# A graph attention layer and its neighbours: the counting of adj spread over 91 steps, the order of chunks in the first and last half head changed, and layer 3's dense stage reordered

## The chip, the cores and the metric

One NeuronCore of one Trainium2 chip. The metric is the device time of one execution in microseconds, as the median of several runs. Engines are named as in the profile: PE (matrix engine; PEld is its weight load), DVE (vector), ACT (scalar, activation functions), POOL (GpSimd), SP (the queue that issues most DMAs).

## The reference

Four graph layers on the same graph, each `x = x + layer(relu(layernorm(x)), adj)`. `x` is 2708 x 512 in float32, `adj` 2708 x 2708 in int32 with zeros and ones, symmetric, with ones on the diagonal. The change concerns layer 2 and the start of layer 3:

```python
def layer2(x, adj, W, a1, a2):           # 8 heads of 64
    Wh = einsum('nd,hdo->hno', x, W)
    f1, f2 = einsum('hno,ho->hn', Wh, a1), einsum('hno,ho->hn', Wh, a2)
    e = leaky_relu(f1[:, :, None] + f2[:, None, :], 0.2)
    att = softmax(where(adj > 0, e, -9e15), axis=-1)
    return elu(einsum('hnm,hmo->hno', att, Wh))   # heads side by side: n x 512

def layer3(x, adj, W_self, b_self, W_nb, b_nb, W_comb, b_comb):
    agg = mask @ x / max(deg, 1)
    both = concatenate([x @ W_self + b_self, agg @ W_nb + b_nb], -1)
    return relu(both @ W_comb + b_comb)
```

Layer 0 is relu of a degree-normalized `adj.T @ X @ W`; layer 1 averages each node's first 64 neighbours and adds a dense part.

## The kernel before, in words

The 2708 nodes are cut into 22 chunks of up to 126 rows (`NC` = 22, `R` = 126; the last one has 62). Layer 0 leaves the transposed adjacency on the chip as int8, six tiles `vT`. Each layer has a dense stage, chunk by chunk (load, normalize, transpose, multiply), and an aggregation over pairs of chunks. All matrix products are in float32 or its one-pass form except where bf16 is named.

**Layer 2, dense** (L655 to L735). `dense` gives load, normalize, transpose, multiply with lags 0 to 3; `product2` multiplies by the weights of all heads, stores the result `wh` to DRAM as `whd`, and multiplies it by the rows `a1` on DVE and `a2` on POOL (L666, L672); `sums2` reduces them to f1 and f2; `rows2` transposes f1 to a row that goes to DRAM (`rT`). `exps2` (L701) takes exp of f2 in two forms on ACT (`ef`, `ec`), and on POOL makes `eb` and splits `ef` and `ef*ec` into three bf16 parts each (`parts`, `parts2`): 13 small operations, once for the first 11 chunks (`EARLY`) during the dense stage and once for the rest in attention.

**Layer 2, attention** (L803 to L1019). The eight heads are ten units: the first and last head are cut in two halves of the target nodes (1384 and 1324 columns), the others have all 2708. Each unit has 22 steps, one per source chunk m: 220 steps. The softmax's weights are factored, so that a step is

- `make` (L858, DVE): `t2 = max(rb, ec) * vT`, one instruction over all columns, into one of four tiles; up to three steps ahead;
- `scale` (L831, L833, ACT): the step's 64 columns of Wh times `ef`, as `whs`; for the chunks not in `BY_SIDE` also a column for the sum of weights;
- `compare` (L843, ACT), only for the 13 chunks in `BY_SIDE` (m % 5 in 1, 3, 4): from `t2` a 0/1 pattern `b` in bf16 by a steep sigmoid;
- `multiply` and `multiply_sides` (L882, PE): `av += whs.T @ t2` in 4 column groups of 32; the sums of weights from `t2` in float32 (chunks not in `BY_SIDE`), or from `b` with `parts` in bf16 (the others), the latter one step later.

`load_wh` fetches three chunks' slices of `whd` at a time, six steps ahead. Work beside the steps is put behind step numbers in `plan`: loads and exp of the next head's row `rb` (L642, L649), `evict` of a unit's results to DRAM (`avT`, `sumT`) at its end, and `count_neighbors` (L932) behind steps 66 to 78, one chunk of `BY_SIDE` each: four ACT conversions of a quarter of the chunk's int8 adjacency to bf16 (L941), into tiles of the x ring (six), and eight matmuls (L946) with `parts2`. The last steps get layer 3's first loads and turns.

**Layer 3, dense** (L747 to L801, L1022 to L1061). For chunk c: `load3` (aT, sT and x from DRAM), `turn3` (sums_ps L766 and av_ps L770 on PE; then rs and y on DVE, L772 to L777), `elu3` (z on POOL L784; th and z with tanh and exp on ACT L787, L788; L785, L789, L790 on DVE), `save3` (x to DRAM from ACT's queue), `normalize3` (statistics L187, L189, square root on ACT L191, L192 and hn L201 on DVE), `transpose3` (hT_ps L210 on PE, hT L212 on ACT), `product3` (nb_ps and self_ps, L182 on PE; halves L249, L251; y L1045, stored from ACT's queue). `staged` runs them in one program order with lags 0, 1, 2, 3, 4, 4, 5 for load, turn, elu, normalize, save, transpose, multiply.

The order of instructions on each engine is fixed when the program is built: a list scheduler starts from the program order above and from its own costs, and semaphores are added where engines meet. Within an engine the instructions run in that order, a waiting one holds up what stands behind it.

Of the kernel before, what the change touches and what calls it, by code (L numbers as in the profile page):

```python
# [44 lines left out]
def fast_layers(  # L45
# [59 lines left out]
    KMAX = max(sizes)  # L105
    EARLY = NC // 2
# [152 lines left out]
    def load_x(src, c, name="x", pool=None, bufs=6, twice=False):  # L259
        n = rows(c)  # L260
        t = (pool or common).tile([P, D], F32, name=name, bufs=bufs)
        if twice and c == NC - 1:
            nc.gpsimd.memset(t[:R], 0.0)
            move(nc.sync, t[TAIL : TAIL + n, :], src[c * R : c * R + n, :])
        move(nc.sync, t[:n], src[c * R : c * R + n, :])
        return t
# [383 lines left out]

    l2p = ctx.enter_context(ExitStack())
# [49 lines left out]
    def exps2(cs):  # L701
        nc.scalar.activation(ef[:, cs], f12[:R, cs, H:], AF.Exp)
        nc.scalar.activation(ec[:, cs], f12[:R, cs, H:], AF.Exp, scale=SLOPE2 - 1.0)
        nc.gpsimd.tensor_scalar(eb[:, cs], ec[:, cs], -STEEP * ABOVE, None, op0=ALU.mult)
        size = cs.stop - cs.start
        rest = cp.tile([R, EARLY, H], F32, name="rest")[:, :size]
        for i, e in enumerate((ef, ec)):
            if i:
                nc.gpsimd.tensor_tensor(rest, ec[:, cs], ef[:, cs], ALU.mult)
                e = rest  # L710
            else:
                e = ef[:, cs]
            for k in range(3):
                part = parts_of[:, cs, :, 3 * i + k]
                nc.gpsimd.tensor_copy(part, e)
                if k < 2:
                    nc.gpsimd.tensor_tensor(rest, e, part, ALU.subtract)
                    e = rest
        nc.gpsimd.tensor_copy(
# [6 lines left out]
    def rows2(c):  # L726
# [4 lines left out]
        if c == NC - 4:  # L731
            exps2(slice(0, EARLY))
            exp_row(*units[0])

    staged(NC, *dense(x2, product2, False, [(4, sums2), (5, rows2)], scalar=True))  # L735

    ws = load_weight(weights, fused[0], "wfs", tag="w")
    wn = load_weight(weights, fused[1], "wfn", tag="w")
# [5 lines left out]
    kept3 = {}  # L744

# [57 lines left out]
    with ExitStack() as stack:  # L803
        at = stack.enter_context(tc.tile_pool(name="att", bufs=1, reuse_waits="tile"))
        weight, wh, whs, acc, sides = {}, {}, {}, {}, {}
        steps = [(u, m) for u in range(len(units)) for m in range(NC)]


        GROUP = 3

        def load_wh(s):
            u, m = steps[s]
            h = units[u][0]
            t = at.tile([R, GROUP, O], F32, name="wh", bufs=3)
            k = min(GROUP, NC - 1 - m)
            if k > 0:
                src = whd[m * R : (m + k) * R, h * O : (h + 1) * O]
                nc.sync.dma_start(t[:, :k], src.rearrange("(k p) o -> p k o", p=R))
            if k < GROUP and m + k == NC - 1:
                src = whd[(NC - 1) * R :, h * O : (h + 1) * O]  # L820
                nc.sync.dma_start(t[:last_rows, k], src)
            for j in range(GROUP):
                wh[u, m + j] = t[:, j]

        def scale(s):

            u, m = steps[s]
            h, q = units[u][0], rows(m)
            t = at.tile([R, O + S], F32, name="whs", bufs=4)
            by = ef[:q, m, h : h + 1]  # L830
            nc.scalar.activation(t[:q, :O], wh.pop((u, m))[:q], AF.Copy, scale=by)  # L831
            if m not in BY_SIDE:
                nc.scalar.activation(t[:q, O:], one6[:q], AF.Copy, scale=by)  # L833
            whs[s] = t
# [43 lines left out]
        def four(out, size, operands, m):  # L878

            for p, (a, b) in zip(out, pieces(size)):  # L880
                for j, (lhsT, rhs, part) in enumerate(operands):
# [4 lines left out]
                        start=(m == 0),  # L886
                        stop=(m == NC - 1),
                    )

        def multiply(s):  # L890
# [3 lines left out]
            if m == 0:  # L894
# [6 lines left out]
            four(acc[u][0], half, [(cols[j % 2], t, j // 2) for j in range(4)], m)  # L901
            if m not in BY_SIDE:
                four(acc[u][1], quarter, [(cols[2], t, j) for j in range(4)], m)

        def multiply_sides(s):

            if s in sides:
# [5 lines left out]
                four(acc[u][1], sizes_of(u)[1], [(w, b, j) for j in range(4)], m)  # L913
# [18 lines left out]
        def count_neighbors(i):  # L932
            m = BY_SIDE[i]
            q = rows(m)
            g, k = where[m]
            if i == 0:
                counted.extend(ps.tile([P, 512], F32, name="adj_sums", tag="ps") for _ in pieces(quarter))
            masks = []
            for j in range(4):
                t = common.tile([P, D], F32, name="x", bufs=6).bitcast(BF16)  # L940
                nc.scalar.copy(t[:q, :quarter], vT[g][:q, k, j * quarter : (j + 1) * quarter])  # L941
                masks.append(t)
            w = parts2[:q, m]
            for p, (a, b) in zip(counted, pieces(quarter)):
                for j, t in enumerate(masks):
# [3 lines left out]
                        t[:q, a:b],  # L949
# [5 lines left out]
            for p, (a, b) in zip(counted, pieces(quarter)):  # L955
                t = common.tile([P, D], F32, name="out", tag="t", bufs=3)
                for j in range(4):
# [4 lines left out]
                    )  # L962

# [14 lines left out]
        behind(5, load_row1, *units[1])  # L978
        behind(6, exp_row, *units[1])
# [8 lines left out]
        for i in range(len(BY_SIDE)):  # L988
            behind(3 * NC + i, count_neighbors, i)

        end = len(steps)
        for c in range(3):
            behind(end - 14 + 2 * c, load3, c)
            behind(end - 6 + 2 * c, turn3, c)
        behind(end - 5, elu3, 0)
        behind(end - 3, normalize3, 0)
        behind(end - 3, elu3, 1)
# [3 lines left out]
        for s in range(-3, len(steps)):  # L1001
            for i in ([0, 3] if s == -3 else [s + 6]):
                if i < len(steps) and (i % NC) % GROUP == 0:
                    load_wh(i)
            if s + 3 < len(steps):
                scale(s + 3)
# [16 lines left out]
    with ExitStack() as stack:  # L1023
# [9 lines left out]
        def skip(fn, first):  # L1033

            return lambda c: fn(c) if c >= first else None

        def product3(c, xc, hT, size):
            n = rows(c)
            pn = ps.tile([P, D], F32, name="nb3_ps", tag="ps")
            product(pn, hT, wn, size)  # L1040
            h3[c] = halves(ring, pn, c)
# [700 lines left out]
```

## Time and profile before

| what | us |
|---|---|
| median of 3 runs | 1899.61 (1892.21, 1899.74, 1899.61) |
| profiled execution | 1893.48 |
| its span, first to last instruction | 1891.6 |
| layer 2's dense stage, first hT_ps to last wh_ps | 818.5 to 911.7 |
| attention, first to last matmul of a step | 919.1 to 1478.5 |
| layer 3's dense stage, first nb_ps to last self_ps | 1491.1 to 1662.7 |

Times of the profile come from the one profiled execution and count from the span's start. A row of a group has: line, engine, operation, what it writes and reads, shapes, count, busy time, mean of one. A row of a timeline has: start, duration, engine and line, operation, tiles, and in brackets the idle time of the engine before it and what ended it. A row of the busy times by stretch has: the stretch and its length, busy time of PE, PEld, DVE, ACT, POOL with counts, the granted PE clock (1.00 is full), the mean share of the DMA engines, and GB/s. In the profile `t2` is shown as `t`, `nb3_ps` as `nb_ps`.

### The profile page before, as it was taken

The numbers are of one execution on the slowest core, as the hardware profiler recorded it, in microseconds if no ns is written. First come the engines' busy times: TensorE is split into PE (matmuls) and PEld (weight loads), VectorE is DVE, ScalarE is ACT, GpSimd is POOL, SyncE is SP. The second block draws the span as 40 slices with busy tenths as digits, with TensorE's granted clock in tenths as the row PEclk, the third lists the DMA queues.
The fourth block names the chain that finished last, engine by engine and source line by source line (L and its number), as shares of the span: only waits on it lengthen the run. The fifth ranks groups of instructions, "written<-read, shape, count | busy, mean of one in ns | idle before, by whom it ended". The sixth has DMA issues, their size and how long they took to land.

```text
span 1891.6 us, 30561 instructions
## 1 busy us (share of the span) xinstructions
PE 1801.5 (95%) x11670; PEld 1061.5 (56%) x11670; DVE 1289.1 (68%) x1812; ACT 903.2 (48%) x1533; POOL 280.9 (15%) x461
## 2 busy tenths in 40 slices
PE   8999899989999999989899999999999799999998
PEld 4556666664446888744344453444444355478886
DVE  4655677784444556766799979999999776524333
ACT  2445777772110000047587898767777766400000
POOL 0101232331111111237600000000000222100000
PEclk9999999999999999989999999999999899999999
DMA  6333455542223111243311212211211444302321
GB/s 221 115 87 96 140 149 154 142 117 73 75 68 97 44 44 47 76 136 107 101 46 34 57 46 57 59 39 29 59 31 41 123 137 137 97 20 81 115 65 41
DMA packets 126041, 160.92 MB, mean 85 GB/s; under 512 B 57406, under 2 KB 77994, under 8 KB 125002
## 3 DMA queue, kind: packets, MB, share of 16 engines
q1 hardware_dynamic: 106764, 123.40, 22.8%
q10 hardware_dynamic: 18544, 33.37, 5.3%
q0 software_dynamic: 576, 2.10, 0.3%
q8 instruction: 94, 1.54, 0.3%
q14 instruction: 63, 0.52, 0.1%
HBM read 111.23 MB, written 47.42 MB: 84 GB/s over the span
## 4 chain that ended last, share of the span: by engine, by line
PE 74%; DVE 7%; DMA 5%; issue 5%; ACT 5%; POOL 2%; SPq 0%; ACTq 0%; DVEq 0%; POOLq 0%
PE acc L330 27%; PE av L882 15%; PE nb_ps L182 8%; PE sums L882 5%; DVE t L858 4%; PE self_ps L182 4%; PE line_ps L182 4%; PE h_ps L182 4%; PE wh_ps L182 3%; DMA ai<-in_adj 2%; PE hT_ps L210 2%; DMA x<-x 1%; DVE cum L418 1%; POOL x L492 1%; ACT sign L428 1%
## 5 line engine op out<-in xcount | busy, mean ns | idle before, releaser
L858 DVE SCALAR_TENSOR_TENSOR t<-rb,ec,vT 126x2708 f32<-126x2708 f32 (+2 forms) x220 | 528.1, 2467 | 25.2 <-ACT b L843 11.0
L882 PE MATMUL av<-t,whs 126*32 126x451 f32 (+4 forms) x4576 | 443.1, 518 | 8.6 <-ACT whs L831 7.4
L330 PE MATMUL acc<-halves,kt 126*126 126x512 f32 x1848 | 430.5, 394 | 1.1 <-DVE kt L1096 1.1
L330 PEld LDWEIGHTS acc<-halves,kt 126*126 126x126 f32 x1848 | 344.0, 186 | 85.6 <-DVE kt L1096 1.2
L843 ACT ACTIVATE b<-t,eb 126x2708 bf16<-126x2708 f32 (+5 forms) x130 | 272.5, 2096 | 39.5 <-DVE t L858 38.4
L882 PEld LDWEIGHTS av<-t,whs 126*32 126x32 f32 (+1 forms) x4576 | 170.6, 110 | 202.0 <-issue 159.8
L330 PE MATMUL acc<-halves,ar 126*126 126x512 f32 x924 | 254.1, 415 | 8.9 <-ACT ab L413 4.3
L330 PEld LDWEIGHTS acc<-halves,ar 126*126 126x126 f32 x924 | 166.5, 189 | 52.8 <-issue 11.6
L563 DVE SCALAR_TENSOR_TENSOR kt<-lastr,index,vT 126x504 fp32r<-126x504 int16 (+1 forms) x132 | 104.3, 798 | 82.1 <-PE acc L330 81.8
L1096 DVE CAST kt<-vT 126x504 fp32r<-126x504 int8 (+1 forms) x132 | 52.7, 400 | 140.8 <-PE acc L330 140.8
L191 ACT ACTIVATE ln_rs<-ln_mv,eps 126x1 f32<-126x1 f32 x88 | 25.5, 294 | 257.6 <-DMA x<-x 202.8
L418 DVE TENSOR_TENSOR_SCAN cum<-ai,deg 126x504 int16<-126x504 int32 (+2 forms) x110 | 125.0, 1143 | 26.9 <-DMA ai<-in_adj 13.9
L784 POOL TENSOR_SCALAR z<-y 126x512 f32<-126x512 f32 x22 | 43.1, 1957 | 646.6 <-DVE y L777 578.2
L428 ACT ACTIVATE sign<-cum,limit 126x504 bf16<-126x504 int16 (+3 forms) x132 | 88.5, 671 | 59.2 <-DVE cum L418 53.9
L882 PE MATMUL sums<-t,whs 126*32 126x339 f32 (+3 forms) x1152 | 107.7, 455 | 5.7 <-ACT out L921 5.7
L831 ACT ACTIVATE whs<-wh,ef 126x64 f32<-126x64 f32 x220 | 73.7, 341 | 69.4 <-PE sums L882 35.5
L212 ACT ACTIVATE hT<-hT_ps 128x504 f32<-128x504 f32 x88 | 51.4, 587 | 103.4 <-PE hT_ps L210 99.4
L187 DVE BATCH_NORM_STATS2 ln_st<-x 126x6 f32<-126x512 f32 x88 | 60.4, 687 | 58.2 <-DMA x<-x 46.0
L468 ACT CAST vT<-vT_ps 126x504 int8<-126x504 f32 (+1 forms) x132 | 70.9, 539 | 47.4 <-DVE sums L459 24.1
L182 PE MATMUL nb_ps<-wn,hT 128*126 128x512 f32 x176 | 81.9, 609 | 2.6 <-ACT hT L212 2.6
L182 PE MATMUL wh_ps<-w2s,hT 128*126 128x512 f32 (+1 forms) x176 | 80.9, 603 | 0.0
L182 PE MATMUL nb_ps<-wfn,hT 128*126 128x512 f32 x176 | 80.4, 600 | 0.0
(172 smaller groups left out, 2054.2 us busy)
## 6 DMA issues: line engine op xcount, KB each, us to landing
x<-x SPq DMA_DIRECT2D x105, 252.0 KB
x<-x ACTq DMA_DIRECT2D x84, 252.0 KB
ai<-in_adj SPq DMA_DIRECT2D x84, 248.1 KB
x<-in_x SPq DMA_DIRECT2D x42, 252.0 KB
rb<-rT SPq DMA_DIRECT2D x7, 1332.8 KB
wh<-whd SPq DMA_DIRECT2D x70, 94.5 KB
whd<-wh SPq DMA_DIRECT2D x21, 252.0 KB
aT<-avT SPq DMA_DIRECT2D x21, 252.0 KB
```

The source lines that it names most:

```text
L182: nc.tensor.matmul(po[:n], lhsT[:, f, :n], w[:, f, :], start=(f == 0), stop=(f == NF - 1))
L187: nc.vector.bn_stats(st[:n], xc[:n])
L330: nc.tensor.matmul(acc[:R], weight[:, k * R : (k + 1) * R], parts[:, i, :], start=(m == 0 and i == 0), stop=(m == NC - 1),)
L418: nc.vector.tensor_tensor_scan(cum[:n, :gw], ai[:n, :gw], ai[:n, :gw], 0.0 if g == 0 else deg[:n, m : m + 1], op0=ALU.add, op1=ALU.max,)
L428: nc.scalar.activation(sign[:n, :gw], cum[:n, :gw], AF.Sign, bias=limit[:n], scale=-1.0, accum_out=signs[:n, m, g : g + 1],)
L468: nc.scalar.copy(vT[g][:, :, m * R : (m + 1) * R], pt[:R, :K, :R])
L563: nc.vector.scalar_tensor_tensor(by_chunk(kt, cs), lastr[:, cs[0] * R : (cs[-1] + 1) * R].rearrange("p (c r) -> p c r", r=R), index[:R, m ...
L831: nc.scalar.activation(t[:q, :O], wh.pop((u, m))[:q], AF.Copy, scale=by)
L843: nc.scalar.activation(b[:q, : hi - lo], weight[s][:q, : hi - lo], AF.Sigmoid, bias=eb[:q, m, h : h + 1], scale=STEEP,)
L858: nc.vector.scalar_tensor_tensor(t[:q, : hi - lo], row[h][:q, lo:hi], ec[:q, m, h : h + 1], vT[g][:q, k, lo:hi], op0=ALU.max, op1=ALU.mult,)
L882: nc.tensor.matmul(p[j * S : j * S + lhsT.shape[1], : b - a], lhsT, rhs[:, part * size + a : part * size + b], start=(m == 0), stop=(m == ...
L1096: nc.vector.tensor_copy(by_chunk(kt, cs), pattern(m, cs))
```

## The change

- `count_neighbors` is split: `mask(i, j)`, one conversion, stands behind step 50 + 7i + j, and the matmuls behind step 55 + 7i, for i from 0 to 12: steps 50 to 139.
- The chunks' order (`orders`): in the first unit 0, 2, 5, 7, 10, then 1, 3, 4, 6, 8, 9, then 11 to 21; in the last unit the 13 chunks of `BY_SIDE` first and the nine others at the end. The matmuls' start and stop flags follow the step's place in its unit.
- `wh` and `whs` move to a pool that is open in the dense stage; `wh` is fetched in pairs (`GROUP` 2, two DMAs where the pair isn't adjacent); the first three loads are issued at dense step NC - 4, the first three `scale` at NC - 2.
- `exps2` uses DVE in place of POOL.
- The loads of layer 3's two weights stand behind step 20 in place of the end of the dense stage.
- The last steps: turn3, elu3, normalize3 and transpose3 of chunk 0 and turn3 of chunk 1 are put there.
- Layer 3's dense stage: one loop with nb3 and self3 apart and the other chunks' work between them.

```diff
+    early = sorted(range(EARLY), key=lambda m: m in BY_SIDE)
+    orders = {
+        0: early + list(range(EARLY, NC)),
+        len(units) - 1: sorted(range(NC), key=lambda m: m not in BY_SIDE),
+    }
+    steps = [(u, m) for u in range(len(units)) for m in orders.get(u, range(NC))]
+    GROUP = 2
...
-        nc.gpsimd.tensor_scalar(eb[:, cs], ec[:, cs], -STEEP * ABOVE, None, op0=ALU.mult)
+        nc.vector.tensor_scalar(eb[:, cs], ec[:, cs], -STEEP * ABOVE, None, op0=ALU.mult)
...
-                nc.gpsimd.tensor_copy(part, e)
+                nc.vector.tensor_copy(part, e)
...
         if c == NC - 4:
             exps2(slice(0, EARLY))
             exp_row(*units[0])
+            for i in range(0, 6, GROUP):
+                load_wh(i)
+        if c == NC - 2:
+            for i in range(3):
+                scale(i)
 
     staged(NC, *dense(x2, product2, False, [(4, sums2), (5, rows2)], scalar=True))
-
-    ws = load_weight(weights, fused[0], "wfs", tag="w")
-    wn = load_weight(weights, fused[1], "wfn", tag="w")
...
+        def mask(i, j):
             m = BY_SIDE[i]
             q = rows(m)
             g, k = where[m]
+            t = masks[i, j] = common.tile([P, D], F32, name="x", bufs=XBUFS).bitcast(BF16)
+            nc.scalar.copy(t[:q, :quarter], vT[g][:q, k, j * quarter : (j + 1) * quarter])
...
-            behind(3 * NC + i, count_neighbors, i)
+            s = 2 * NC + 6 + 7 * i
+            for j in range(4):
+                behind(s + j, mask, i, j)
+            behind(s + 5, count_neighbors, i)
 
         end = len(steps)
-        for c in range(3):
-            behind(end - 14 + 2 * c, load3, c)
-            behind(end - 6 + 2 * c, turn3, c)
-        behind(end - 5, elu3, 0)
-        behind(end - 3, normalize3, 0)
-        behind(end - 3, elu3, 1)
+        for at_step, fn, c in (
+            (14, load3, 0),
+            (12, load3, 1),
+            (8, turn3, 0),
+            (7, load3, 2),
+            (6, elu3, 0),
+            (5, normalize3, 0),
+            (4, turn3, 1),
+            (2, transpose3, 0),
+        ):
+            behind(end - at_step, fn, c)
...
-        stages = (
-            (0, load3, 3),
-            (1, turn3, 3),
-            (2, elu3, 2),
-            (3, normalize3, 1),
-            (4, save3, 0),
-            (4, transpose3, 0),
-            (5, multiply3, 0),
-        )
-        staged(NC, *((lag, skip(fn, first)) for lag, fn, first in stages))
+        elu3(1)
+        normalize3(1)
+        turn3(2)
+        save3(0)
+        for c in range(NC):
+            do(load3, c + 3)
+            if c:
+                do(normalize3, c + 1)
+            nb3(c)
+            if c:
+                do(transpose3, c + 1)
+                do(turn3, c + 2)
+            self3(c)
+            if c == 0:
+                transpose3(1)
+            do(elu3, c + 2)
+            do(save3, c + 1)
```

`nb3` and `self3` are the two halves of `product3`; `do` leaves out chunks past the last one.

## The prediction

> **What bounds the kernel now.** I read the page's first part, then the busy times by stretch over layers 2 and 3, then the timelines of single engines there, since the change touches only the end of layer 2's dense stage, the attention and layer 3's dense stage.
>
> ```profile
> span 1891.6 us, 30561 instructions
> PE 1801.5 (95%) x11670; PEld 1061.5 (56%) x11670; DVE 1289.1 (68%) x1812; ACT 903.2 (48%) x1533; POOL 280.9 (15%) x461
> ```
>
> PE looks like the bound everywhere. By stretch it is not (columns: PE, PEld, DVE, ACT, POOL, granted clock, DMA):
>
> ```profile
> 1060.00:1140.00 80.00, 71.96 (x800) 39.74 (x804) 62.55 (x21) 77.05 (x105) 0.00 (x0) 0.94 0.18 46
> 1140.00:1220.00 80.00, 80.00 (x964) 32.30 (x960) 79.91 (x28) 61.80 (x69) 0.00 (x0) 1.00 0.22 61
> 1478.00:1491.00 13.00, 4.97 (x24) 3.94 (x24) 10.77 (x29) 11.01 (x16) 5.03 (x3) 0.50 0.43 115
> 1491.00:1663.00 172.00, 171.74 (x538) 85.50 (x536) 106.86 (x262) 99.23 (x137) 35.03 (x20) 0.99 0.40 123
> ```
>
> Attention runs at the pace of DVE and PE together (second row). Where adj is counted (first row) ACT is full and both wait. Between attention and layer 3 (third row) PE does 5 of 13 us at half clock. In layer 3's dense stage (fourth row) PE never waits. DVE's timeline in the counting stretch shows the wait in brackets, and the conversions' group shows why:
>
> ```profile
> 1101.40 5.99 DVE L858 SCALAR_TENSOR_TENSOR t<-rb,ec,vT 126x2708 f32<-126x2708 f32 x2 [2.27 <-ACT b L843]
> 1110.42 5.99 DVE L858 SCALAR_TENSOR_TENSOR t<-rb,ec,vT 126x2708 f32<-126x2708 f32 x2 [3.03 <-PE sums L882]
> L941 ACT CAST x<-vT x52: 740/755/762, 873.1 to 1120.0; 126x677 bf16<-126x677 int8 x48, 62x677 bf16<-62x677 int8 x4
> ```
>
> One chunk of layer 3 now, followed through the timelines of DVE, POOL and ACT: its first result y at 1526.00, its normalized rows hn at 1540.69.
>
> ```profile
> 1526.00 0.69 DVE L777 TENSOR_TENSOR y<-av_ps,rs 126x512 f32<-126x512 f32 x1
> 1526.78 1.99 POOL L784 TENSOR_SCALAR z<-y 126x512 f32<-126x512 f32 x1 [5.95 <-DVE y L777]
> 1529.50 0.63 ACT L787 ACTIVATE th<-z 126x512 f32<-126x512 f32 x1
> 1530.16 0.63 ACT L788 ACTIVATE z<-z 126x512 f32<-126x512 f32 x1
> 1530.82 0.69 DVE L789 SCALAR_TENSOR_TENSOR z<-z,th 126x512 f32<-126x512 f32 x1 [1.91 <-ACT z L788]
> 1532.11 0.68 DVE L790 TENSOR_TENSOR x<-x,z 126x512 f32<-126x512 f32 x1
> 1532.82 0.31 ACTq L99 DMA_DIRECT2D x<-x  x1
> 1533.17 1.28 ACT L191 ACT_TABLE_LOAD   x1 [0.50 <-DVE rs L773]
> 1534.46 0.29 ACT L191 ACTIVATE ln_rs<-ln_mv,eps 126x1 f32<-126x1 f32 x1
> 1535.57 0.16 DVE L192 RECIPROCAL ln_rs<-ln_rs 126x1 f32<-126x1 f32 x1
> 1540.69 0.54 DVE L201 TENSOR_SCALAR hn<-x,ln_mv,ln_rs 126x512 f32<-126x512 f32 x1
> ```
>
> Eleven rows on three engines, each needing the one above it, with idle time between them that hurts nobody: the stages' lags (turn3 1, transpose3 4) put three whole chunks of PE work between a chunk's av_ps and its hT_ps. PE's own timeline gives nb_ps 3.44, self_ps 3.43, sums_ps and av_ps 0.61, hT_ps 0.43, together 7.91 us a chunk, and its nb_ps start 7.91 us apart; so the cover is 23.7 us.
>
> **What the Trainium skill says.** "ScalarE: Activation LUTs", What ACT_TABLE_LOAD costs: 1283 ns a load plus about 1380 ns of drain. The trace agrees on 1.28 us; it shows no drain (the load at 1534.45 is followed by its activation after 0.01), so I take 1.28. The same page, Table sets: exp and tanh share a set, sqrt has another; here th and z follow without a load, ln_rs has one. "TensorE: Matmul & The Clock Gate", Part 1: an idle window of about 3.4 us halves the clock. The trace agrees: half clock after gaps of 7.38 us (911.69), 4.08 (1059.82) and 3.74 (1124.55), none after 1.62 (1277.09). "SBUF — State Buffer", two separate sides: a DVE instruction with two SBUF inputs and a GpSimd instruction exclude each other; z takes 1.99 us beside DVE's x, 1.48 alone (1473.91).
>
> **The change, part by part**, against the profiled execution (1893.48 us, span 1891.6; the median of the runs, 1899.61, is 6.1 above it).
>
> *Entry to attention.* exps2 goes from POOL to DVE: 13 small operations for each half. On POOL the first half holds up wh_a and stops PE once, for 1.12 us before 887.93: gone. On DVE no row shows them; the nearest are the rs operations, 0.14 to 0.20, so I take 0.2 each (not below nothing, since DVE must do them). The first half's 2.6 us lie in the dense stage, where DVE is busy 59 of 93 us; the second half stands in DVE's queue before and between the first t2, where every matmul waits: +2. PE's wait for wh<-whd (the chain: transfer from 914.54, first av at 919.07) goes, since load_wh and scale are issued in the dense stage on SP and ACT, both with slack there; but the first t2, from 916.52 plus 1.65, is next: -1. In the order 0, 2, 5, 7, 10, 1, 3, 4, 6, 8, 9 six 0/1 chunks follow each other, 1.43 (b) + 0.34 (whs) of ACT each against 1.57 of DVE, with the row's exp (1.31 and two loads) among them: 1 to 3 us of stalls, against the 1.2 and 1.8 that DVE's timeline shows before 942.77 and 955.65 now: nothing. wh in pairs, 110 tiles for 80, costs SP more issues of 0.3 to 0.4 us, six steps ahead; the eight weight issues that go behind step 20 had no waiter: nothing. Sum -1 (-4 to +3).
>
> *adj over 91 steps.* Full steps follow each other every 2.95 us on DVE. In the counting stretch the brackets of its t2 rows are 0.77, 2.10, 0.54, 1.24, 1.55, 2.27, 3.03, 1.78, 0.59 and 3.42: 17.3 us, lost to 52 conversions x 0.755 = 39 us of ACT in 13 steps. Spread, they add 9.4 us to each 22 steps, where ACT has 13 x 2.55 (b) + 22 x 0.34 + 9 x 0.31 (whs) + 7.5 (row with two loads 5.0, five evictions 2.5) = 51 of 65: 93% with them. The order written by the scheduler still puts most in fours (3.0 us). The 0.29 us of matmuls each (eight, in four column groups) now come where PE has 64.2 of 64.9 us in a unit: +1. I leave 3 us of stalls: -13 (-17 to -6).
>
> *End of attention.* The last unit's first t2 starts at 1436.67, the first nb_ps at 1491.08: 54.4 us. In it lie 3.8 us in which sums waits for a b that stands behind elu3 on ACT, and 6.2 in which hT_ps waits. After: 13 t2 x 1.51 = 19.6 us for the 0/1 chunks; then nine steps with sums in the matmul, each 1.67 on PE (24 passes of 0.07) against 1.51 on DVE, with turn3(0), (1) and (2), 0.61 each. No b is left for elu3 to delay. I walked the order of the engines from the end of t2 number 13, with the durations above: turn3(0) done at 5.6; y(0), behind t2 number 20 on DVE, 12.1; z(0) 14.2 to 15; th, load, exp to 16.8; the last step's whs, behind them on ACT, 17.5; z, x, statistics to 19.3; hn(0), behind turn3(1)'s results on DVE, 21.8; hT_ps(0), which stands inside the last step on PE and blocks it, 22.3; nb3(0) 23.8. So 43.4 instead of 54.4: -11 (-14 to -6). load3(2) moves from 10 steps before the end to 7; its three issues on SP are still over 10 us ahead of turn3(2), and landing takes about 4 (whd above 4.11): nothing.
>
> *Layer 3's loop.* On PE's order: nb3(c), hT_ps(c+1), sums_ps and av_ps(c+2), self3(c), nb3(c+1), hT_ps(c+2). So a chunk's chain has only self3 + nb3 = 6.87 us of cover. The chain, each with its hop: sums end to y start 0.95, y 0.69, z 2.07, th 0.67, exp 0.67, z 0.74, x 0.72, then on ACT's queue the issue of x3 (0.34; it waits for x and stands before the table load), load 1.31, ln_rs 0.31, reciprocal 0.19, hn 0.58, to PE 0.14: 9.4. hT_ps (0.43) and sums_ps (0.29) lie between the chain's start and the previous one's end: period 10.1 against 7.91, PE idle 2.2 a chunk. hT_ps(3) to hT_ps(21), 18 periods: +39. Before that the same walk gives waits of 1.7, 0.7 and 2.1: +4.5. Sum +44 (30 if the load escapes the issue and the period is 9.4; 48 if z takes 2.2 on POOL). The waiting instruction is hT_ps; behind it on PE stand the next turn and self3, so the delay feeds itself.
>
> Sum: -1 - 13 - 11 + 44 = **+19 us**.
>
> **The rivals**, from 1896.5, the middle of profiled execution and median. (1) *The chain fits* (ends faster): if sums_ps to hT_ps takes at most 7.2 us, which the 6.87 of cover and av_ps's lead hide, the loop keeps 7.91 and only the entry's waits stay: -1 - 13 - 11 + 4 = -21, 1875. For: DVE is busy 107 and ACT 99 of 172 us there, so nothing else stands in the way. Against: even with issue and load free the statistics (0.94) take their place and the sum is 8.7. 8%. (2) *The load is hidden*: the chain is 8.7, the period 9.4, the loop +30, in all +5: 1901. For: loads start before their input is there (1524.94, statistics at 1525.80). Against: each of them starts 0.03 us after the issue that stands before it. 17%. (3) *Gaps halve the clock*, or ACT at 93% stalls as it does now: about +15 more (one window of 3.4 us at half clock, 1.7 us, in every other chunk; or the 13 given back), 1931. For: a gap in every chunk. Against: each is 2.2, and 1.62 did nothing. 15%. That the change does nothing is excluded by the engines' orders. The forecast: 60%.
>
> **The numbers.** From the profiled execution 1912.5, from the median 1918.6; I take 1915. The range reaches from rival 2 less the 4 us by which the entry and the counts may do better to rival 3: 1897 to 1932; rival 1 and half of rival 3's upper side are left out. Beyond 0.5% (9.5 us, about what a measurement of this kernel can tell from no change) lie: slower 0.57 of the forecast's 0.60, rival 3's 0.15 and 0.03 of rival 2, 0.75; same 0.03 + 0.14 = 0.17; faster rival 1, 0.08.
>
> **What would show it.** Right: hT_ps waits for hn about 2 us in each chunk, nb3 starts every 10 us, PE's share in layer 3's dense stage falls from 100% to near 80%; no DVE waits over 1 us from step 70 to 86; first nb3 some 43 us after the last unit's first t2. Wrong: nb3 every 7.9 us (then rival 1), a clock of 0.5 in that stage (rival 3), or a counting stretch that still loses over 10 us.

## The result and the profile after

The changed kernel takes 1945.86 us (median of four runs, 1940.79 to 1947.54) where before takes 1897.97 (1892.21 to 1899.74): a ratio of 1.0253, 95% interval 1.0223 to 1.0283. It is 48 us slower; the forecast was 1915, and its range ended at 1932. The first lines of the page of the changed kernel:

```profile
span 1944.6 us, 30558 instructions
PE 1813.8 (93%) x11670; PEld 1068.1 (55%) x11670; DVE 1309.8 (67%) x1838; ACT 901.4 (46%) x1532; POOL 259.3 (13%) x435
```

PE has the same 11670 matmuls and only 12 us more of busy time, so most of the loss is waiting. To see where, I took the same marks from both traces: the first wh_ps of layer 2's dense stage, the first t2, the last unit's first t2, the first nb_ps of layer 3 and the end of its last self_ps.

| stretch | before | after | difference | forecast |
|---|---|---|---|---|
| first wh_ps to first t2 (entry) | 95.3 | 102.0 | +6.7 | -1 |
| to the last unit's first t2 (adj) | 520.1 | 521.8 | +1.7 | -13 |
| to the first nb_ps (end of attention) | 54.4 | 45.8 | -8.6 | -11 |
| to the end of the last self_ps (layer 3's loop) | 171.5 | 219.8 | +48.2 | +44 |
| to the end | 229.0 | 229.2 | +0.2 | 0 |
| sum | 1070.4 | 1118.6 | +48.2 | +19 |

The sum of the differences agrees with the difference of the medians (47.9). Ahead of the first mark lie layers 0 and 1, which the change leaves alone. They took 821.2 us before and 826.0 after in these two executions, and between 816.5 and 826.0 in all fourteen traces of this document, so I count this as no effect of the change. The stretches vary too: in the runs below that leave a stretch of the changed kernel as it is, adj takes 519.7 to 523.8 us and the loop 219.4 to 223.7.

Two rows of the busy times by stretch answer to those shown of before: attention with the counting in it, and layer 3's loop (columns: PE, PEld, DVE, ACT, POOL, granted clock, DMA).

```profile
1002.00:1346.30 344.30, 330.75 (x3931) 153.66 (x3924) 324.77 (x111) 267.90 (x311) 0.00 (x0) 0.98 0.17 47
1495.60:1715.40 219.80, 177.67 (x554) 85.46 (x552) 131.12 (x288) 104.86 (x144) 40.84 (x23) 0.99 0.35 102
```

In the first, 344.3 us where before has 344.9 (988.9 to 1333.8), DVE is idle for 19.5 and PE for 13.5 of them, with ACT busy 78%: as many waits are left as before, in other places. In the second PE does 177.7 of 219.8 us, 81%, where it had 100%. PE's waits in that loop, added up by what ended them (total, times, longest), have one large row, which before does not have at all:

```profile
PE hT_ps L211 <- DVE hn L202: 40.2, 19, 3.1
PE hT_ps L211 <- DVE ln_rs L193: 1.3, 1, 1.3
PE nb_ps L183 <- ACT hT L213: 0.7, 1, 0.7
```

The timeline of all engines shows one period of that loop (the bracket is the idle time before a row and what ended it). It is the chain that the prediction added up, from the end of sums_ps at 1540.99 to the next hT_ps at 1550.39:

```profile
1540.24 0.62 PE L211 MATMUL hT_ps<-ident,hn 126*128 126x126 f32 x4 [2.05 <-DVE hn L202]
...
1540.70 0.29 PE L814 MATMUL sums_ps<-mix,sT 80*126 80x16 f32 x2
...
1541.96 0.69 DVE L825 TENSOR_TENSOR y<-av_ps,rs 126x512 f32<-126x512 f32 x1
...
1542.74 1.99 POOL L832 TENSOR_SCALAR z<-y 126x512 f32<-126x512 f32 x1 [8.16 <-DVE y L825]
...
1544.76 0.63 ACT L835 ACTIVATE th<-z 126x512 f32<-126x512 f32 x1 [1.97 <-POOL z L832]
...
1546.80 0.69 DVE L838 TENSOR_TENSOR x<-x,z 126x512 f32<-126x512 f32 x1
...
1547.53 0.31 ACTq L99 DMA_DIRECT2D x<-x  x1
...
1547.87 1.28 ACT L192 ACT_TABLE_LOAD   x1 [1.83 <-DMA s<-y]
...
1549.17 0.29 ACT L192 ACTIVATE ln_rs<-ln_mv,eps 126x1 f32<-126x1 f32 x1
...
1549.69 0.55 DVE L202 TENSOR_SCALAR hn<-x,ln_mv,ln_rs 126x512 f32<-126x512 f32 x1
...
1550.39 0.41 PE L211 MATMUL hT_ps<-ident,hn 126*128 126x126 f32 x2 [2.05 <-DVE hn L202]
```

It takes 9.40 us from the end of sums_ps to the start of hT_ps, and 10.15 from hT_ps to hT_ps: the forecast said 9.4 and 10.1.

### The profile page after: what moved, and what is told of

Its sections match the earlier page's. It is cut to its first block, busy times and chain, and to the rows that moved or that the text cites. A ratio compares the mean times of both kernels' runs of the same rounds, so it can differ in the third digit from the quotient of the medians.

```text
span 1944.6 us, 30558 instructions
## 1 busy us (share of the span) xinstructions
PE 1813.8 (93%) x11670; PEld 1068.1 (55%) x11670; DVE 1309.8 (67%) x1838; ACT 901.4 (46%) x1532; POOL 259.3 (13%) x435
## 4 chain that ended last, share of the span: by engine, by line
PE 58%; DVE 13%; issue 10%; DMA 9%; ACT 6%; POOL 2%; SPq 0%; ACTq 0%; DVEq 0%; POOLq 0%
PE acc L331 27%; PE av L901 9%; DVE t L877 8%; PE nb_ps L183 5%; PE line_ps L183 4%; DMA ai<-in_adj 4%; PE self_ps L183 3%; PE wh_ps L183 3%; PE sums L901 3%; DMA rb<-rT 2%; DMA s<-y 2%; PE hT_ps L211 2%; DVE cum L419 1%; ACT L192 1%; DMA x<-x 1%
## 5 line engine op out<-in xcount | busy, mean ns | idle before, releaser
L901 PE MATMUL av<-t,whs 126*32 126x451 f32 (+4 forms) x4576 | 452.6, 519 | 20.7 <-ACT out L940 11.8
L331 PE MATMUL acc<-halves,ar 126*126 126x512 f32 x924 | 258.3, 421 | 8.9 <-ACT ab L414 4.2
L832 POOL TENSOR_SCALAR z<-y 126x512 f32<-126x512 f32 x22 | 44.3, 2016 | 714.0 <-DVE y L825 714.0
L901 PE MATMUL sums<-t,whs 126*32 126x339 f32 (+3 forms) x1152 | 115.5, 457 | 1.6 <-ACT out L940 1.6
L211 PE MATMUL hT_ps<-ident,hn 126*128 126x126 f32 x352 | 55.6, 283 | 54.0 <-DVE hn L202 45.7
L211 PEld LDWEIGHTS hT_ps<-ident,hn 126*128 126x128 f32 x352 | 41.3, 146 | 89.6 <-issue 73.3
```

Of the source, the lines that this page charges most:

```text
L211: nc.tensor.transpose(pt[:, f, :n], hn[:n, f * P : (f + 1) * P], ident[:n, :n])
L331: nc.tensor.matmul(acc[:R], weight[:, k * R : (k + 1) * R], parts[:, i, :], start=(m == 0 and i == 0), stop=(m == NC - 1),)
L901: nc.tensor.matmul(p[j * S : j * S + lhsT.shape[1], : b - a], lhsT, rhs[:, part * size + a : part * size + b], start=(s % NC == 0), stop=( ...
```

## Theories

Three stretches, three causes, to be taken apart one at a time.

*Loop*: the chain of 9.4 us has 6.87 us of cover. Its rivals are filled queues, transfers and the lower clock.

*adj*: the forecast's reason for a loss here was ACT at 93%. The trace says something else. Nearly all the lost time lies behind the fourth t2 of units 3 to 6 (steps 69, 91, 113 and 135, units counted from 0): the next t2 starts 5.7, 6.6, 3.1 and 4.4 us later than the usual 2.95. The first of them, all engines:

```profile
1068.18 3.38 PE L901 MATMUL av<-t,whs 62*32 62x451 f32 x32
...
1069.67 1.28 ACT L650 ACT_TABLE_LOAD   x1
...
1071.48 0.31 PE L901 MATMUL sums<-b,parts 62*32 62x338 bf16 x1
1073.37 2.46 ACT L650 ACTIVATE rb<-rb 126x2708 f32<-126x2708 f32 x1 [2.41 <-DMA rb<-rT]
...
1076.18 1.38 ACT L940 COPY out<-av 128x451 f32<-128x451 f32 x3
...
1076.74 3.24 PE L901 MATMUL av<-t,whs 126*32 126x452 f32 x16 [4.95 <-ACT out L940]
...
1084.39 3.04 DVE L877 SCALAR_TENSOR_TENSOR t<-rb,ec,vT 126x2708 f32<-126x2708 f32 x1 [5.63 <-PE av L901]
```

PE waits for an eviction of the unit that has just ended, and DVE in turn for PE. The pool `ps` has eight tiles of one bank (L120). A unit takes three for av and two for sums, adj_sums takes two. The counting now runs from step 55 to 139, over four units' ends, with one bank free where the next unit wants three. The trace shows that one bank: a step's av is 24 matmuls, eight for each tile, and the 32 in the first row are the last step's 24 and eight of the new unit, in the one free tile. The second tile waits; so it does at the other three ends. Before, the counting ran within one unit, from 66 to 78, and the new unit's 24 all ran ahead of any wait for an eviction. At a unit's end without it, before has the same order on ACT (the row's exp, then the evictions), and PE has no gap there:

```profile
1208.78 2.46 ACT L649 ACTIVATE rb<-rb 126x2708 f32<-126x2708 f32 x1 [1.12 <-DMA rb<-rT]
...
1211.60 1.39 ACT L921 COPY out<-av 128x451 f32<-128x451 f32 x3
```

So my theory for adj became: two banks held. The Trainium skill, "PSUM — Partial Sum Buffer", section PSUM: the matmul accumulator, gives the size of the resource: 8 banks of 2 KiB per partition. No run here measures that size; the kernel's eight tiles agree with it. The rival stays ACT's load.

*Entry*: PE waits twice for f in the dense stage (2.31 and 2.69 us). The theory is exps2 in DVE's queue; the rival is the whs and wh issues that moved there.

Changes of time below are against the changed kernel, minus for faster: a kernel's ratio to before less 1.0253, times the before that was measured with it (1893 to 1896 us). The stretches are those of the table.

## Experiments on layer 3's loop

**lags**: before's stages, started from the state that the last head leaves.

```diff
...
-        for c in range(NC):
-            do(load3, c + 3)
...
-            do(save3, c + 1)
...
+        stages = (
+            (0, load3, 3), (1, turn3, 2), (2, elu3, 1), (3, normalize3, 1),
+            (4, save3, 0), (4, transpose3, 1), (5, multiply3, 0),
+        )
+        staged(NC, *((lag, skip(fn, first)) for lag, fn, first in stages))
```

> The changed kernel with layer 3's dense stage again in the six lagged stages of before (turn3 lag 1, elu3 2, normalize3 3, transpose3 4, multiply3 5), started from what the last head has already done. Theory (the chain of 9.4 us from sums_ps to hT_ps has 6.87 us of cover): with three chunks of cover hT_ps waits nowhere, nb_ps follows nb_ps every 7.91 us, first nb_ps to last self_ps takes 171 to 175 us instead of 219.8, the time is 1946 - 46 = 1900 (1895 to 1906). Rival (the gaps come from queues that the rest of the change has filled, transfers or the lower clock): the period stays above 9.4 us and the time above 1930.

Measured: 1905.5 us against 1892.78, ratio 1.0070 (1.0048 to 1.0093), so 35 us of the 46 expected. The loop is as expected: nb_ps every 7.91 us, 172.5 us in all. What was missed is its start, on PE's timeline:

```profile
1498.20 1.08 PE L818 MATMUL av_ps<-ident,aT 128*126 128x128 f32 x4 [6.25 <-DMA aT<-avT]
1501.33 1.07 PE L211 MATMUL hT_ps<-ident,hn 126*128 126x126 f32 x4 [2.05 <-DVE hn L202]
1502.20 5.76 PE L183 MATMUL nb_ps<-wfn,hT 128*126 128x512 f32 x8
```

The lagged stages put a turn3 whose chunk is not loaded yet, and another chunk's hT_ps, in front of the first nb_ps, which was ready: it comes 57.9 us after the last unit's first t2, not 45.8. The lags cure the loop and throw away what the end of attention had won.

**ahead**: the changed loop with one more chunk between a chunk's turn3 and its hT_ps (elu3(2), save3(1) and load3(3) are issued ahead of the loop).

```diff
         for c in range(NC):
-            do(load3, c + 3)
-            if c:
-                do(normalize3, c + 1)
+            do(load3, c + 4)
+            do(normalize3, c + 2)
+            do(save3, c + 2)
             nb3(c)
-            if c:
-                do(transpose3, c + 1)
-                do(turn3, c + 2)
+            do(transpose3, c + 1)
+            do(turn3, c + 3)
             self3(c)
...
-            do(elu3, c + 2)
-            do(save3, c + 1)
+            do(elu3, c + 3)
```

> The changed kernel with layer 3's loop one chunk further ahead: turn3, elu3 and save3 for the chunk after the one they are now issued for, normalize3 with them; the work of each chunk is the same. Theory (chain of 9.4 us against its cover): the cover becomes 6.87 + 7.91 = 14.8 us, hT_ps waits under 0.3 us in each chunk, nb_ps follows nb_ps every 7.91 us, first nb_ps to last self_ps takes 166 to 173 us (219.8 now), the time falls by 46 to 52 from that of the changed kernel, to the time of before within 6 us. Unlike the lagged stages the last head's lead is kept: first nb_ps 46 us after the last unit's first t2. Rival (queues, transfers, the clock): the period stays above 9.4 us.

Measured: 1898.41 against 1893.00, ratio 1.0031 (1.0015 to 1.0047): -42, a little short of the 46 to 52 expected. After the first period nothing waits any more on PE's timeline (no bracket), and the period is 7.91:

```profile
1506.44 0.60 PE L211 MATMUL hT_ps<-ident,hn 126*128 126x126 f32 x4
...
1510.92 3.60 PE L183 MATMUL nb_ps<-wfn,hT 128*126 128x512 f32 x8
1514.35 0.59 PE L211 MATMUL hT_ps<-ident,hn 126*128 126x126 f32 x4
...
1518.83 3.60 PE L183 MATMUL nb_ps<-wfn,hT 128*126 128x512 f32 x8
```

The first nb_ps comes after 45.3 us: the lead is kept. The loop takes 178.1 and not 166 to 173, since its first period is 14.11: hT_ps(1) waits 3.79 us there, as self3(0) now stands behind it instead of in front. The rival falls: with the same operations, transfers and queues the wait is gone, once there is cover.

**x3_on_sp**: one issue moved.

```diff
-        move(nc.scalar, x3[c * R : c * R + n, :], kept3[c][0][:n])
+        move(nc.sync, x3[c * R : c * R + n, :], kept3[c][0][:n])
```

> The changed kernel with x3 written from SP's queue instead of ACT's. Theory: the issue of x3 waits for x and holds up the table load behind it; without it the load runs beside z and x, the chain is 8.7 us instead of 9.4, the period falls from 10.15 to 9.45 us, the time falls by 12 to 14. Rival 2 of the prediction (the load is hidden or hideable by itself): no change, period 10.15. Rival 3 (ACT's queue is held by the issue of s3 that also stands there): period 9.8 to 10.15, the time falls by under 6.

Measured: 1925.88 against 1893.00, ratio 1.0177 (1.0160 to 1.0194): -14; period 9.45. ACT's timeline shows the load in its new place, over before its activation has its input:

```profile
1540.02 0.31 ACTq L99 DMA_DIRECT2D s<-y  x1
1540.42 1.28 ACT L192 ACT_TABLE_LOAD   x1
1542.83 0.29 ACT L192 ACTIVATE ln_rs<-ln_mv,eps 126x1 f32<-126x1 f32 x1 [1.13 <-DVE ln_mv L190]
```

So the load was on the path only because the issue of x3 stood in front of it in ACT's queue, waiting for x. One moved issue is worth 0.7 us a chunk.

## Experiments on the counting

**no_count_matmuls** and **one_conversion** part the two suspects. The first leaves out the counting matmuls of 12 of the 13 chunks: ACT's work stays, the banks are free, and some 8 us of matmuls leave PE. The second lets all 13 chunks read the first chunk's four conversions: the banks are held and ACT is free.

```diff
         def count_neighbors(i):
+            if i < len(BY_SIDE) - 1:
+                return
```

> The changed kernel without the counting matmuls of 12 of the 13 chunks (their sums are left out of the result); all 52 conversions of adj on ACT stay in their steps, and the two PSUM banks are taken only for the last chunk. Theory (two of eight banks are held over 91 steps, so the next unit has one free bank instead of three and waits for evictions that stand on ACT behind the exp of a row): DVE's stalls at the fourth step of units 3, 4, 5, 6 (5.6, 6.5, 3.0, 4.4 us) fall to under 1 us each, the time falls by 14 to 19 (1927 to 1932). Rival (ACT is too full with the conversions): the stalls stay within 1 us of what they are, the time falls by 0 to 4.

```diff
         def mask(i, j):
+            if i:
+                masks[i, j] = masks[0, j]
+                return
```

> The changed kernel with only the first chunk's four conversions of adj, read by the counting matmuls of all 13 chunks (the counts of 12 chunks are therefore those of the first); matmuls, banks and their 91 steps stay. Theory (banks): the stalls at the fourth step of units 3 to 6 stay above 2 us each, the time falls by at most 6 (1940 to 1946). Rival (ACT's load): they fall to under 1 us each and the time falls by 14 to 19.

Measured: without the matmuls 1930.10 against 1892.78, ratio 1.0196 (1.0165 to 1.0227), -11, short of the 14 to 19 expected. The adj stretch falls by 16.4 us to 505.4, but in this execution layer 3's loop takes 223.7, with four windows of half clock where the changed kernel had one. With one conversion 1939.34, ratio 1.0256 (1.0220 to 1.0292), no change; the stretch takes 523.6. DVE's timeline at the first of the four places, first without the matmuls, then with one conversion:

```profile
1077.52 3.04 DVE L877 SCALAR_TENSOR_TENSOR t<-rb,ec,vT 126x2708 f32<-126x2708 f32 x1 [0.58 <-PE sums L901]
```

```profile
1075.52 11.89 DVE L877 SCALAR_TENSOR_TENSOR t<-rb,ec,vT 126x2708 f32<-126x2708 f32 x4 [5.67 <-PE av L901]
```

With 48 of 52 conversions gone the four stalls are 5.7, 6.9, 3.1 and 6.3 us. ACT's load is not the cause. That it is the banks and not the matmuls' own time on PE, the last run of this section shows, which keeps the matmuls.

**evict_first** asked whether the order on ACT alone would do: it issues the exp of a row behind the three av evictions of the unit that has just ended.

```diff
+        def exp_after(u):
+            with tc.issue_after(evicted[u - 2]):
+                exp_row(units[u][0], 0, N)
```

> The changed kernel with one order forced on ACT: from the fourth head's row on, the exp of a row (with its table load and its wait for the row's transfer) is issued behind the three evictions of the unit that has just ended, not before them. Banks, conversions and their steps stay. Theory (the next unit waits for banks, whose eviction waits for the exp): the stalls at the fourth step of units 3 to 6 (5.7, 6.6, 3.1, 4.4 us) fall to 0.5 to 2.5 each, the time falls by 8 to 15. Rival (the banks alone set it, the order doesn't matter): they stay within 1 us, the time falls by 0 to 3.

Measured: 1940.70 against 1893.00, ratio 1.0249 (1.0231 to 1.0266): no change that can be told from none. The adj stretch falls by 3.9 us to 518.0, and the four stalls are 5.8, 4.7, 3.4 and 3.4; the time was to fall by 8 to 15: a miss. ACT's timeline shows what took the exp's place:

```profile
1068.88 2.55 ACT L862 ACTIVATE b<-t,eb 126x2708 bf16<-126x2708 f32 x1 [2.85 <-DVE t L877]
1071.34 1.39 ACT L946 COPY out<-av 128x451 f32<-128x451 f32 x3
1072.60 0.37 ACT L691 ACTIVATE whs<-wh,ef 126x64 f32<-126x64 f32 x1
1072.99 1.28 ACT L650 ACT_TABLE_LOAD   x1
1074.29 2.46 ACT L650 ACTIVATE rb<-rb 126x2708 f32<-126x2708 f32 x1
```

The evictions now stand behind a b that waits for its t; PE's gap is 4.43 us where it was 4.95. That part of my theory falls: at this place the exp in front of the evictions is not what costs the time. With the banks short, the b that took its place costs nearly as much.

**count_by_unit** and **count_two_adds** count within a unit only and add five groups up in SBUF; the second adds whole tiles.

```diff
+                        start=(i in first_of),
+                        stop=last,
...
+            for p, t, (a, b) in zip(counted, total, pieces(quarter)):
+                for j in range(4):
+                    own = slice(j * S, j * S + 3 * H)
...
+                        nc.vector.tensor_tensor(
+                            t[own, : b - a], t[own, : b - a], p[own, : b - a], ALU.add
+                        )
```

> The changed kernel with the count summed in PSUM within a unit only: five groups of 2 or 3 chunks, each group copied (the first, ACT) or added (the others, 32 small DVE operations in all) to a tile in SBUF, so that no bank is held over a unit's end. Theory (banks held): the stalls at the fourth step of units 3 to 6 go (under 1 us each); DVE's 32 operations of 0.4 to 0.5 us cost 13 to 16 of what is won, since DVE sets the pace: the time falls by 2 to 8. Rival (ACT's load): the stalls stay and the time rises by 10 to 16.

```diff
-                        p[j * S : j * S + 3 * H, : b - a],
+                        p[j * S : (j + 1) * S, : b - a],
...
+                    nc.vector.tensor_tensor(t[:, : b - a], t[:, : b - a], p[:, : b - a], ALU.add)
```

> The changed kernel with the count summed in PSUM within a unit only, as in count_by_unit, but each group added to SBUF in 2 operations over all 128 partitions instead of 8 over 24 each (the matmuls write 32 rows a quarter instead of 24). Theory (the banks cost the stalls; count_by_unit gave them back in 32 additions of 0.50 us on DVE): the stalls stay gone, 8 additions of about 0.5 us cost 4 us, the time falls by 10 to 15 from that of the changed kernel: 1926 to 1931 where before has 1893. Rival (whatever ends at a unit's end costs as much: the stalls are shifted, not removed): 1938 to 1942.

Measured: 1940.68 against 1893.00, ratio 1.0248 (1.0231 to 1.0265), -1, just under the 2 to 8 expected; and 1930.81 against 1894.88, ratio 1.0182 (1.0159 to 1.0205), -13. In both at most 1.0 us is left at the four steps; one step later remain 1.5 us (step 70) in the first and 0.7 and 2.2 (steps 70 and 136) in the second. The adj stretch takes 523.8 us in the first and 510.6 in the second, 11.2 less than in the changed kernel. Both keep all the conversions and all the matmuls; what they change is how long the banks are held. The groups of the additions, in that order (count, busy, mean ns):

```profile
L988 DVE TENSOR_TENSOR total<-total,adj_sums 24x338 f32<-24x338 f32 (+1 forms) x32 | 16.1, 503 | 0.6
```

```profile
L988 DVE TENSOR_TENSOR total<-total,adj_sums 128x338 f32<-128x338 f32 (+1 forms) x8 | 3.7, 500 | 0.0
```

An addition takes 0.50 us over 24 partitions and over 128. On the engine that sets the pace, 32 of them gave back what the banks had won; 8 do not.

## Experiments on the entry, and all together

**pool_exps** puts the small operations back on POOL (`nc.vector` to `nc.gpsimd` in exps2).

> The changed kernel with the 13 small operations of exps2 on POOL again. Theory (on DVE the first half stands in front of the row sums f of layer 2's dense stage, and f_ps waits for f): the two gaps of PE before f_ps (2.31 and 2.69 us) go, at most the 1.1 us of before stays, layer 2's dense stage from first to last wh_ps takes 90.5 us instead of 97.0, the time falls by 6 (1940). Rival (the whs and wh issues that moved into that stage hold it up on ACT and SP): it stays at 96 to 97 us, the time at 1946.

Measured: 1937.06 against 1892.78, ratio 1.0224 (1.0191 to 1.0258), -5.5, which the interval does not tell from none. The stretch does: first to last wh_ps 93.2 us (97.0 changed, 90.5 before), so 3.8 of 6.5. The trace of the changed kernel shows what DVE does there while the next row sum waits:

```profile
880.34 0.37 DVE L760 CAST parts<-ef 126x88 bf16<-126x88 f32 x1 [0.93 <-ACT ef L747]
...
881.09 1.33 DVE L760 CAST parts<-rest 126x88 bf16<-126x88 f32 x1
...
884.50 1.32 DVE L754 TENSOR_TENSOR rest<-ec,ef 126x88 f32<-126x88 f32 x1
...
888.79 0.68 DVE L711 TENSOR_TENSOR wh_a<-wh,arow 126x512 f32<-126x512 f32 x1
```

The thirteen operations take 6.8 us, not 2.6: 0.28 to 0.37 each and three of 0.9 to 1.3. Each of the three runs beside an operation of POOL on wh_a (from 880.85, 884.44 and 885.79). But with exps2 on POOL a gap of 2.43 us stays; ACT's timeline of that run has four whs operations in front of the row's exp and of the wh that f needs:

```profile
878.79 0.33 ACT L691 ACTIVATE whs<-wh,ef 126x64 f32<-126x64 f32 x1
879.03 0.30 ACT L693 ACTIVATE whs<-one,ef 126x32 f32<-126x32 f32 x1
879.24 0.33 ACT L691 ACTIVATE whs<-wh,ef 126x64 f32<-126x64 f32 x1
879.48 0.30 ACT L693 ACTIVATE whs<-one,ef 126x32 f32<-126x32 f32 x1
879.80 1.28 ACT L650 ACT_TABLE_LOAD   x1
```

**entry_back** moved the call of scale behind the dense stage as well.

```diff
-        if c == NC - 2:
-            for i in range(3):
-                scale(i)
...
-            if 0 <= s < len(steps) - 3:
+            if s < len(steps) - 3:
                 scale(s + 3)
```

> The changed kernel with exps2 on POOL again and the first three whs scaled where before has them, behind layer 2's dense stage, not in it. The run with exps2 alone on POOL left a gap of 2.43 us before one f_ps, with four whs operations (1.2 us) on ACT in front of the row's exp and the copy of wh. Theory (queued work on ACT and DVE in the dense stage holds up wh, f and so f_ps): the gap falls to 1.1 us and no half clock follows; first wh_ps to first t2 takes 95 to 96 us (102.0 changed, 98.0 with exps2 on POOL, 95.3 before); the time is 6 to 7 under the changed kernel's: 1934 where before has 1893. Rival (the wh loads on SP, or the order of the 0/1 chunks, which remain): it stays at 98.

Measured: 1940.44 against 1894.88, ratio 1.0238 (1.0217 to 1.0259), -3; first wh_ps to first t2 98.3 us, gap 2.43: a miss. The trace shows why: the whs operations stand where they stood. The place of the call in the source did not set the order here. My reading is that an operation is held back by what it needs, and wh, whs and their space were all there early.

**all_three** adds entry_back, count_two_adds and ahead up, with self3(0) in front of transpose3(1).

> The changed kernel with entry_back, count_two_adds and layer 3's loop one chunk ahead (as in ahead, with self3(0) in front of transpose3(1), which waited 3.8 us there). If the three causes are separate their effects add up: -6.5 - 12 - 49 from the changed kernel (1940 where before has 1893): 1873 (1868 to 1880), faster than both kernels. If one of them only hides another (PE's pace in attention, one more wait at the loop's start) it is 1885 to 1895.

Measured: 1881.97 against 1894.88, ratio 0.9934 (0.9919 to 0.9949): faster than both kernels. The stretches of the table are 96.3, 510.8, 44.3 and 175.4 us, 62.7 less than in the changed kernel, where 67 were expected: 1881.97 lies above the 1868 to 1880 written down, since entry_back had not repaired the entry. The three parts alone gave -42, -13 and -3, together -58; all_three gives -60. So the effects add up. Its page:

```profile
span 1874.7 us, 30581 instructions
PE 1792.6 (96%) x11670; PEld 1049.5 (56%) x11670; DVE 1298.4 (69%) x1820; ACT 894.4 (48%) x1524; POOL 284.3 (15%) x462
```

**all_and_whs_late** holds wh and whs back by their pool. As that pool is open only behind the dense stage, the first calls of load_wh and scale stand there too.

```diff
-        t = cp.tile([R, GROUP, O], F32, name="wh", bufs=3)
+        t = at.tile([R, GROUP, O], F32, name="wh", bufs=3)
...
-        t = cp.tile([R, O + S], F32, name="whs", bufs=4)
+        t = at.tile([R, O + S], F32, name="whs", bufs=4)
```

> The kernel all_three with the tiles wh and whs in the attention's own pool again (as before), whose space is free only when layer 2's dense stage has ended. In entry_back the source put the whs behind the dense stage, and the order written for ACT put them back in front of the row's exp all the same; here the pool holds them back. Theory (in the dense stage four whs operations, 1.2 us of ACT, stand in front of the table load and exp of the row and the copy of wh that f waits for): PE's gap before f_ps falls from 2.4 to 1.1 us and no half clock follows, first wh_ps to last wh_ps takes 90 to 91 us (91.5 with the gap, 97.0 in the changed kernel), first wh_ps to first t2 95 to 96 (96.3 now); PE's wait for wh comes back at the entry, hidden to 0.5 us by the first t2; the time is 1 to 2 us under all_three's ratio of 0.9934. Rival (half clock and gap come from POOL's exps2 alone): gap 2.4 us, no change.

Measured: 1882.56 against 1895.74, ratio 0.9926 (0.9911 to 0.9940): 1.5 us under all_three, which the intervals do not tell from none. The stretch answers: first to last wh_ps 90.5 us, first t2 after 95.3, both as before the change, and on PE's timeline the gap of before:

```profile
892.51 0.27 PE L743 MATMUL f_ps<-ident,f 126*8 126x126 f32 x1 [1.12 <-DVE f L732]
```

So of the entry's 6.7 us 4.0 go with exps2 on DVE (pool_exps), and the rest with the early wh and whs. That rest is 2.7 us in pool_exps, where a window of half clock follows the gap of 2.43, and 1.0 in all_three, with the same gap and no half clock. Whether the pool or the later loads hold the whs back was not separated. The early scaling itself won little: the first av waits 6.74 us for the first t2 in the changed kernel, and waited 7.38 for whs before.

## Why the prediction was wrong, step by step

- **Layer 3's loop, +44: right** in its mechanism and nearly in size, +48.2. Period, chain, the table load behind the issue of x3, and the wait at hT_ps are as written, and three runs confirm them. Of the 4 us missing 2.9 are before's last four periods: they were 7.30, 7.30, 7.30 and 6.87 us, and I had counted 7.91 throughout.
- **End of attention, -11: right**, -8.6. hT_ps(0) comes 41.8 us after the last unit's first t2 (forecast 41.4). Most of the missing 2.4 us is half clock: after hT_ps's wait of 3.11 us the clock is 0.5 from 1491.45 to 1494.87, and hT_ps to nb_ps takes 4.06 us. In the four runs where the clock stayed full there it takes 2.5, against the 1.5 that I had put; the rest of the last step and a turn3 stand between the two on PE.
- **adj over 91 steps, -13: this step failed**, +1.7. Its first half came true: steps 66 to 87 take 70.6 us where they took 83.5, 12.9 less, and of the 70.6 the first new stall is 5.7. The sentence that failed is "I leave 3 us of stalls". I looked for the stalls in ACT's load, and one_conversion shows that this costs nothing. The walk never counted PSUM banks. Two banks held from step 55 to 139 cost 5.7 + 6.6 + 3.1 + 4.4 = 19.8 us at four units' ends; freeing them gives 16.4 of the stretch back without the matmuls, and 11.2 with them and eight additions (count_two_adds). Holding a buffer longer is a cost of its own, even when no operation is added. A hint stood in the profile of before: of the ten waits that the prediction put down to the conversions the first two, 0.77 and 2.10 us, lie ahead of the counting's conversions in that stretch (the first at 1072.1; six had run earlier). They follow PE's wait of 4.08 us up to 1063.90, which an eviction ended and which the prediction read for the clock alone.
- **Entry, -1: failed**, +6.7. "The first half's 2.6 us lie in the dense stage, where DVE is busy 59 of 93 us" took an average over the stage for cover. At that place wh_a and f stand behind it, and f_ps behind f on PE. The size was off too: 6.8 us, not 2.6. And I wrote that whs has slack on ACT there: four of its operations lengthened the one chain on ACT that PE was already waiting for (1.12 us before, 2.43 then). The sum was wrong as well: -1.1, +2 and -1 make 0, not -1. The +2 for the second half of exps2 did not show: the first head's 44 steps, which lie in the row adj, take 74.0 us with it on DVE and 74.1 on POOL (pool_exps). Before they took 72.4; where the 1.6 come from stays open.
- **Rivals.** Rival 3 gave 1931, and for 13 of its 15 us (the counting's gain is lost again) it described the size, but by the wrong cause, ACT; that is luck. Its other cause, half clock in every other chunk of the loop, did not come: one window in the profiled execution. Rival 1 (the chain fits) and rival 2 (the load is hidden) are out: period 10.15; x3_on_sp shows that rival 2 comes true only once the issue is moved.

Open: at the four ends PE waits 4.95, 2.90, 1.20 and 2.80 us for an eviction, 11.9 together, where the stalls sum to 19.8. Half clock (6.8 us of it) follows at the first two and not at the last two; where it does follow at the fourth, as in pool_exps, that stall is 6.4 us and not 4.4 after nearly the same wait (3.02). How the rest splits was not separated. Nor is a wait for an eviction always a loss: with the banks free PE still waits 3.7 us at the first end, behind av and in front of sums, and DVE loses 0.3 (count_two_adds).

## What to carry to other kernels

For every buffer that a change holds longer, count who else allocates from that pool while it is held; spreading work out in time spreads its accumulators too. Cover must be looked up at the place, in the queue of the engine that gets the work, not in a stage's average. In a software pipeline compare the chain from a stage's output to its next use with the matmuls between the two: one more chunk of lead was worth 42 us here, and an issue that waits in front of a table load was worth 14.

## What the runs showed of the hardware that I had not expected

The clock fell to half after gaps of only 2.05 us, in some chunks and not in others with the same gap. The Trainium skill, "TensorE: Matmul & The Clock Gate", Part 1, says that the window is free-running and 3413 ns long. The traces agree (in each, all clock changes lie on a grid of 3.413 us, within 0.004) and show how full a window must be. I took each window of full clock from 60 us on, without the last of a trace, in all fourteen traces, and the share of it in which PE was busy. Under 0.4 the next window had half clock in 97 of 97 cases; from 0.4 to 0.6 in 39 of 220; above 0.6 never, in over 7000. What decides between 0.4 and 0.6 stays open. A gap of 2.05 us leaves 0.40 of a window that it lies in whole, and more of each when it straddles two. So it halves the clock only now and then (one period of 11.80 in the changed kernel, two of 11.8 with exps2 on POOL). My prediction took a gap as long as a window for the condition; that is too long.
